# The first batch's v by quarters, with the preparation of the weights dealt out anew

## Chip, core and metric

The kernel runs on one core of a Trainium2 chip. The metric is the device time of one execution in microseconds; before the change it is 2723.61 us, the median of 3 runs (2723.01 to 2725.67).

## What is computed

The input x has shape (4, 1024, 32, 32) in float32: four batches of 1024 channels by 1024 tokens. Two layers follow each other. The first is attention over tokens, the second three convolutions with batch norms. The change lies in the first:

```
qkv = x @ w_qkv.T + b_qkv            # q, k, v: 1024 x 1024 weights each
q, k = rms_norm(rope(q)), rms_norm(rope(k))      # norm over all 1024 features
attn = softmax(q @ k.T * 64 ** -0.5)             # 16 heads of 64
out = rms_norm((attn @ v) @ w_proj.T) + x
```

So each batch has four products of 1024 x 1024 by 1024 x 1024: q, k, v and, after attention, the projection, called y in the kernel. Everything is float32. The second layer is 1x1, 3x3 and 1x1 convolution, each with a batch norm over all batches, and a residual.

## The kernel before

**Order of the stages.** The loop over b (L1000) takes one batch at a time through q, k, v, attention and y. The second layer follows after the last batch. In the profiled execution the stages of the first batch begin at 5 us (q), 103 (k), 204 (v), 319 (attention) and 554 (y); those of the second at 639 (q), 725 (k), 812 (v) and 897 (attention).

**One level and two levels.** The products of 1024 x 1024 matrices use a scheme of Strassen's kind: a matrix is cut into 2 x 2 blocks, and 7 products of blocks replace 8, at the price of sums of blocks ahead of the products (S1 to S4 of the weights, as many of the data) and of sums of results behind them. `project` (L290) does this once: 7 block products, each in 4 groups of output rows, so 28 steps. For q and k such a step is 4 matmuls with 512 columns; for v, which is wanted with tokens on the partitions (`tokens`), it is 16 matmuls with 128 columns each (L309 to L315). The profile counts each float32 matmul as two records. `project2` (L452) does it twice: each of the 7 outer products (their operands are listed in OUTER) is again done by 7 products of quarters, so 49 steps of 4 matmuls with 256 columns. Before the change the first batch's q, k and v use `project`; all else uses `project2`.

**The weights for two levels.** Each outer product k of `project2` needs seven weight quarters. Three are read as they are (`quarter`, L389); four are sums that were made once and stored in DRAM, in `wd2` (L147). A *weight part* is the making of these for one weight and one k (`prepare`, L400): four loads of 256 KB, four sums of 128 x 512 on VectorE (DVE), four stores of 256 KB through POOL's queue. Outer operands other than A11, A12 and A22 are themselves sums of blocks, which are read from `wd` (L145). In the first batch `operands` (L224), called by `project` for each of its 4 groups, loads four blocks through SP's queue, makes these sums on DVE, uses them for its own product, and stores them in `wd` through POOL's queue. For the projection's weights `prepare_blocks` (L416) makes them alone, in four steps.

**When the parts are made.** There are 28 weight parts (four weights, seven k). Before the change they are dealt out over the first batch:
- first q: q's and v's parts 0, 1, 6 and k's 0, 6, in the free tile `unused` (L1011)
- first k: q's 2, 3, 4, 5, in `room`, the tile that v will fill (L1021)
- first v: k's 1 to 5, in the half of x that v's products no longer need (L1029)
- first attention: four block sums and seven parts of the projection's weights, and v's 2, 3, 4, 5 (L1037)

In the projection stages a part is run by `weight_parts` (L966): loads through POOL's queue at a set point, sums `lag` steps later. The clock for this is `pace["at"]`, which `product_done` (L257) moves by 1 for each step of `project` and by 0.5 for each of `project2`. In attention a part is an `extra` step: after each of the 16 head pairs (two halves of the queries, eight pairs of heads each) one step is popped (L821 to L824), which makes the sums of the part loaded before and loads the next, through SP's queue, into four chunks of the weight ring.

**Other queues and buffers.** `wring` (L157) is a ring of 8 chunks of 256 KB for weights. It serves the matmuls' weights, `operands`, and the parts made in attention. A chunk is loaded again when the work on it, stores included, has ended. DVE also does the rotations (`turn`, L724), eight per q or k after the norm; each has two operations of 128 x 1024 and two accumulating DMAs on POOL's queue (L734). They wait in `waiting` and are taken out as the pace allows. `rest` (L272) takes out what is left before attention: in the first batch all of it, later all but 4, which are then taken out after the first head pairs. The instructions of TensorE, DVE, ScalarE (ACT) and POOL keep the order of the program; those of SP are ordered by the framework.

`in_place` (L659) gives `project2` its rooms for the sums of the data: parts of the destination at first, of x later. `project2` with `first` makes the sums of its first outer product itself (L542).

Of the kernel before, what the change touches and what calls it, by code (L numbers as in the profile page):

```python
# [12 lines left out]
AF = mybir.ActivationFunctionType  # L13
ALU = mybir.AluOpType
# [71 lines left out]
def program(ctx, tc, x, wblk, w2, w3, vecs, cos, sin, out, bad):  # L86
# [66 lines left out]
    with tc.tile_pool(name=f"st{u}", bufs=2) as st, ExitStack() as s:  # L153
# [58 lines left out]
        def chunk(name):  # L212
            return wring.tile([P, NH, P], F32, tag="w", name=name)

        def flat(t):
            return t.rearrange("p a b -> p (a b)")
# [6 lines left out]

        def operands(b, base, g, name):  # L224


            at = base // NT * NG + g
            if b > 0:
                out = [chunk(f"w_{name}_{o}") for o in SUMS]
                for o, t in enumerate(out):  # L230
                    nc.sync.dma_start(flat(t), wd[at, o])
                return out + [block(base, g + NG, 1, f"{name}_21")]
            a11, a12 = (block(base, g, ih, f"{name}_1{ih}") for ih in range(2))
            a21, a22 = (block(base, g + NG, ih, f"{name}_2{ih}") for ih in range(2))
            s1 = chunk(f"w_{name}_s1")
            nc.vector.tensor_tensor(s1, a21, a22, ALU.add)
            nc.vector.tensor_tensor(a21, a11, a21, ALU.subtract)
            nc.vector.tensor_tensor(a11, s1, a11, ALU.subtract)
            nc.vector.tensor_tensor(a12, a12, a11, ALU.subtract)
            spend(4 * TT)  # L240
            for o, t in enumerate((a11, s1, a21, a12)):
                nc.gpsimd.dma_start(wd[at, o], flat(t))
            return [a11, s1, a21, a12, a22]
# [45 lines left out]

        def project(b, base, bs, ts, outs, bias, squares, tokens, tag, w1=None):  # L290

# [8 lines left out]
            def product(o, w, name, first, last):  # L300
                r = right[name]
                if not tokens:
                    for i in range(NH):
                        nc.tensor.matmul(
                            o, w[:, i, :], r(i), start=first and i == 0, stop=last and i == NH - 1,
                            skip_group_check=True,
                        )
                    return
                for t in range(CH // P):  # L309
                    at = slice(t * P, (t + 1) * P)  # L310
                    for i in range(NH):
                        nc.tensor.matmul(
                            o[:, at], r(i)[:, at], w[:, i, :], start=first and t == 0 and i == 0,
                            stop=last and i == NH - 1, skip_group_check=True,
                        )  # L315

            def shaped(o):
                return o.rearrange("p (t f) -> p t f", f=P) if tokens else o

            def take(out, o, c):  # L320

                if bias is None or c is None:
                    nc.scalar.copy(out, shaped(o))
                else:
                    nc.scalar.activation(out, o, AF.Identity, bias=col(bias, c))

            def add(out, o, c):
                spend(TT)
                if bias is None:
                    nc.vector.tensor_tensor(out, shaped(o), out, ALU.add)  # L330
                else:
                    nc.vector.scalar_tensor_tensor(out, o, col(bias, c), out, ALU.add, ALU.add)

            def add_sbuf(out, t):
                spend(TT)
                nc.vector.tensor_tensor(out, shaped(t), out, ALU.add)

# [8 lines left out]
            for g in range(NG):  # L346
                c11 = outs(g)[0]
                o2 = bank("o2", f"pb_{tag}_{b}_{g}")
                product(o2, w1[NG + g], "A12", True, True)
                after(1, lambda o2=o2, c11=c11, g=g: add(c11, o2, g))  # L350
                after(2, lambda c11=c11: squares(c11, 0))
                product_done()
                if g == 1:
                    w2[0] = operands(b, base, 0, f"{tag}_{b}_0b")
            for g in range(NG):
# [8 lines left out]
                p5 = temp(f"p5_{n}")  # L364
                nc.scalar.activation(p5, o2, AF.Identity, bias=col(bias, g + NG)) if bias else nc.scalar.copy(p5, o2)
                product_done()
                if g + 1 < NG:
                    w2[g + 1] = operands(b, base, g + 1, f"{tag}_{b}_{g + 1}b")
                product(o, w[2], "S3", False, False)
# [29 lines left out]

        def prepare(which, base, k, alloc, queue=nc.sync):  # L400

# [13 lines left out]

        def prepare_blocks(base, g, alloc, queue=nc.sync):  # L416

# [171 lines left out]
        def qk_proj(b, base, bs, ts, bias, dst, tag, w1=None, two=None, bias_later=False):  # L589
# [22 lines left out]
            if two is None:  # L612
                project(b, base, bs, ts, outs, bias, squares, False, tag, w1)
                return total
# [15 lines left out]
            return total  # L630

        def v_proj(b, bs, ts, v, two=None):

            if two is not None:
                project2(b, 1, WV, *two, v, True, "v", lambda c: None)
                return

            def outs(g):
                n = N // P // 2
                return [  # L640
                    v[:, c * n : (c + 1) * n, f * P : (f + 1) * P] for f in (g, g + NG) for c in range(NCH)
                ]

            project(b, WV, bs, ts, outs, None, lambda *a, **k: None, True, "v")

# [128 lines left out]
        def attention(b, c, q_all, k_all, v, probs_, late, ready, extra, slow):  # L774
# [4 lines left out]
            for hp in range(NHP):  # L779
# [39 lines left out]
                if slow:  # L819
                    slow.pop(0)()  # L820
                if waiting:  # L821
                    next_waiting()
                elif extra:
                    extra.pop(0)()  # L824
# [141 lines left out]
        def weight_parts(parts, first, step, lag, alloc):  # L966

            for i, (which, base, k) in enumerate(parts):

                def begin(which=which, base=base, k=k):  # L970
                    after(lag, prepare(which, base, k, alloc, nc.gpsimd))

                after(first + i * step, begin)

        def pieces_of(tile, cols=NCH):

            at = deque(tile[:, i, h] for i in range(NT) for h in half[:cols])

            def alloc(name):
                at.rotate(-4)  # L980
                return [at[i] for i in range(-4, 0)]

            return alloc

        vector_and_act = {mybir.EngineType.DVE, mybir.EngineType.Activation}
# [14 lines left out]
        for b in range(B):  # L1000
# [8 lines left out]
            if b == 0:  # L1009
                unused = kp.tile([P, NT, N], F32, tag="k", name="unused")  # L1010
                parts = [(which, base, k) for which, base in ((0, WQ), (1, WV)) for k in (0, 1, 6)]  # L1011
                parts += [(3, WK, k) for k in (0, 6)]
                weight_parts(parts, 8, 2.4, 4, pieces_of(unused))
            tq = qk_proj(b, WQ, xs[b], ts[b], "bq", q_all, "q", w1 if b == 0 else None, two, True)
            rope(b, q_all, tq, eps_q, HD / C, None, "q", b == 0)
# [4 lines left out]
            if b == 0:  # L1020
                parts = [(0, WQ, k) for k in (2, 3, 4, 5)]  # L1021
                weight_parts(parts, 2, 5, 4, pieces_of(room))
            tk = qk_proj(b, WK, xs[b], ts[b], "bk", k_all, "k", None, two)
            rope(b, k_all, tk, eps_rms, 1.0 / C, (wqk_other, wqk), "k")
            v = room
            if b == 0:

                free = pieces_of(xs[b][:, :, half[0]], 1)
                weight_parts([(3, WK, k) for k in range(1, len(OUTER) - 1)], 8.5, 3, 3, free)  # L1029
            v_proj(b, xs[b], ts[b], v, (*two2[2], False) if b > 0 else None)  # L1030

            rest(leave=4 if b > 0 else 0)
            psum_for("att")

            todo = []
            if b == 0:
                todo = [lambda g=g: prepare_blocks(WP, g, pieces) for g in range(NG)]  # L1037
                todo += [
                    lambda which=which, base=base, k=k: prepare(which, base, k, pieces)
                    for which, base, ks in ((2, WP, (0, 1, 6, 2, 3, 4, 5)), (1, WV, (2, 3, 4, 5)))  # L1040
                    for k in ks
                ]
            made = []

            def extra_step():
                if made:
                    made.pop()()
                if todo:
                    made.append(todo.pop(0)())

# [48 lines left out]
            else:  # L1099
                back = {1: x_tile(b + 1)}  # L1100
                for i in range(NT):
                    after(8 + 1.5 * i, lambda i=i: read_back(1, (i,)))
            yt[b] = kp.tile([P, NT, N], F32, tag="k", name=f"y_{b}")
            two = (2, *in_place(q_all, tc_, yt[b], False), True)
# [357 lines left out]
```

## Time and profile before

| what | value |
|---|---|
| median of 3 runs | 2723.61 us |
| profiled execution: its time, its span | 2724.17 us, 2722.3 us |
| mean granted TensorE clock | 0.996 |
| DMA | 442.84 MB, mean 163 GB/s |
| DVE line L802 (sums of the softmax) | 470.4 us in 384 instructions |
| ACT line L798 (exponentials) | 476.2 us in 512 instructions |
| first v, records of 128 columns, 896 | from 204.26 us to attention at 319.05 us |
| second v, records of 256 columns, 392 | from 811.58 us to attention at 897.42 us |

The span is from the first to the last instruction of the one profiled execution; the execution's own time is 1.87 us longer. An instruction's duration is from its own start to its end, and matmuls overlap in the array: their rate is read from start to start. Idle time stands ahead of the instruction that ended it, with what released it. The releaser is inferred from semaphores.

### The profile page before, as it was taken

The numbers are of one execution on the slowest core, as the hardware profiler recorded it, in microseconds if no ns is written. First come the engines' busy times: TensorE is split into PE (matmuls) and PEld (weight loads), VectorE is DVE, ScalarE is ACT, GpSimd is POOL, SyncE is SP. The second block draws the span as 40 slices with busy tenths as digits, with TensorE's granted clock in tenths as the row PEclk, the third lists the DMA queues.
The fourth block names the chain that finished last, engine by engine and source line by source line (L and its number), as shares of the span: only waits on it lengthen the run. The fifth ranks groups of instructions, "written<-read, shape, count | busy, mean of one in ns | idle before, by whom it ended". The sixth has DMA issues, their size and how long they took to land. (4 is left out here: it accounts for less than half of the span.)

```text
span 2722.3 us, 33404 instructions
## 1 busy us (share of the span) xinstructions
PE 2679.2 (98%) x11914; PEld 1684.0 (62%) x11914; DVE 2129.7 (78%) x2461; ACT 1088.2 (40%) x1507; POOL 444.4 (16%) x536
## 2 busy tenths in 40 slices
PE   9999899999999999999999999999999999999997
PEld 4449633378888433588886333888884335846843
DVE  5565599988797877888888877887888878646987
ACT  2221255523343555433343555233425654312266
POOL 3553323210011121100111211100111211000000
PEclk9999999999999999999999999999999999999999
DMA  7896745576677332356666330665783323672165
GB/s 272 318 279 182 233 155 167 155 221 197 181 189 210 83 78 47 113 169 220 181 186 168 70 71 17 201 197 180 189 232 90 64 46 122 188 255 85 62 224 210
DMA packets 238399, 442.84 MB, mean 163 GB/s; under 512 B 27728, under 2 KB 111232, under 8 KB 238224
## 3 DMA queue, kind: packets, MB, share of 16 engines
q1 hardware_dynamic: 197280, 304.17, 35.7%
q0 software_dynamic: 40944, 136.44, 19.1%
q8 instruction: 98, 1.61, 0.2%
q14 instruction: 77, 0.63, 0.1%
HBM read 305.97 MB, written 96.78 MB: 148 GB/s over the span
## 5 line engine op out<-in xcount | busy, mean ns | idle before, releaser
L802 DVE TENSOR_TENSOR den<-den,p 128x1024 f32<-128x1024 f32 x384 | 470.4, 1225 | 41.4 <-ACT p L798 1.4
L798 ACT ACTIVATE p<-sc 128x1024 f32<-128x1024 f32 x512 | 476.2, 1043 | 53.7 <-PE sc L791 53.6
L791 PE MATMUL sc<-q,k 64*128 64x512 f32 x2048 | 457.9, 596 | 1.9 <-ACT p L798 1.2
L791 PEld LDWEIGHTS sc<-q,k 64*128 64x128 f32 x2048 | 190.1, 186 | 267.3 <-issue 121.1
L808 PE MATMUL cx<-p,to 128*64 128x512 f32 x1536 | 340.2, 595 | 0.0
L808 PEld LDWEIGHTS cx<-p,to 128*64 128x64 f32 x1536 | 106.0, 137 | 228.3 <-issue 228.3
L772 POOL TENSOR_SCALAR q<-q,vec 128x512 f32<-128x512 f32 x64 | 127.4, 1996 | 561.0 <-DVE q L771 561.0
L478 PE MATMUL p_y<-q,w_y 128*128 128x256 f32 x928 | 209.8, 379 | 0.0
L478 PEld LDWEIGHTS p_y<-q,w_y 128*128 128x128 f32 x928 | 176.0, 190 | 27.1 <-issue 3.4
L813 ACT COPY q<-cx 128x512 f32<-128x512 f32 x64 | 37.5, 587 | 357.0 <-PE cx L808 357.0
L473 PE MATMUL p_v<-w_v,x 128*128 128x256 f32 x696 | 157.9, 379 | 1.8 <-DVE x L444 1.7
L478 PE MATMUL p_k<-to,w_k 128*128 128x256 f32 x672 | 153.1, 381 | 3.2 <-ACT to L567 3.2
L478 PE MATMUL p_q<-to,w_q 128*128 128x256 f32 x672 | 152.5, 380 | 0.1
L800 DVE TENSOR_TENSOR den<-p 128x1024 f32<-128x1024 f32 x64 | 76.5, 1195 | 89.3 <-ACT p L798 89.3
L473 PEld LDWEIGHTS p_v<-w_v,x 128*128 128x128 f32 x696 | 132.0, 190 | 20.8 <-DVE x L444 3.0
L478 PEld LDWEIGHTS p_k<-to,w_k 128*128 128x128 f32 x672 | 126.7, 190 | 24.3 <-ACT to L567 5.6
L478 PEld LDWEIGHTS p_q<-to,w_q 128*128 128x128 f32 x672 | 127.2, 190 | 19.6 <-ACT q L532 1.3
L837 DVE RECIPROCAL rec<-dn 128x512 f32<-128x512 f32 x32 | 107.2, 3351 | 20.4 <-PE dn L831 20.3
L808 PE MATMUL cx<-p,rq 128*64 128x512 f32 x512 | 113.4, 595 | 0.0
L1366 PE MATMUL c<-h,w 128*128 128x512 f32 x256 | 110.3, 592 | 0.9 <-ACT h L1268 0.9
L734 POOL DMA_DIRECT2D k<-ks x64 | 56.9, 1099 | 243.1 <-ACT p L798 95.8
L478 PE MATMUL p_y<-to,w_y 128*128 128x256 f32 x384 | 90.1, 379 | 0.0
(475 smaller groups left out, 4264.0 us busy)
## 6 DMA issues: line engine op xcount, KB each, us to landing
w_y<-wd2f SPq DMA_DIRECT2D x112, 256.0 KB
w_q<-wd2f SPq DMA_DIRECT2D x84, 256.0 KB
w_k<-wd2f SPq DMA_DIRECT2D x84, 256.0 KB
w_v<-wd2f SPq DMA_DIRECT2D x84, 256.0 KB
x<-in_x_dram SPq DMA_DIRECT2D x64, 256.0 KB
q<-qs POOLq DMA_DIRECT2D x64, 256.0 KB, 5.5
k<-ks POOLq DMA_DIRECT2D x64, 256.0 KB, 4.5
inv<-rec SPq DMA_DIRECT2D x256, 64.0 KB
```

What stands on the lines that cost most here:

```text
L473: nc.tensor.matmul(o[:, q].rearrange("p (g f) -> p g f", g=2), r[:, i, q * P : (q + 1) * P], wt[:, :, i, :], skip_group_check=True, **at,)
L478: nc.tensor.matmul(o[:, q], wt[:, q, i, :], r[:, i, :], skip_group_check=True, **at)
L734: nc.gpsimd.dma_start(dst[i::2, f, :], other[1 - i :: 2, :], accum_op=ALU.add)
L772: nc.gpsimd.tensor_scalar(cx, cx, col("bv", hp), None, ALU.add)
L791: nc.tensor.matmul(sc[:, j], k_all[d, hp, t * P : (t + 1) * P], q_all[d, hp, at], start=True, stop=bad is not None,)
L798: nc.scalar.activation(p, sc, AF.Exp)
L800: nc.vector.tensor_tensor(d_, probs[0], p, ALU.add)
L802: nc.vector.tensor_tensor(d_, d_, p, ALU.add)
L808: nc.tensor.matmul(o[j * HD : (j + 1) * HD, :], v[:, t, h0 : h0 + HD], probs[t][:, j], start=(t == 0), stop=(t == N // P - 1),)
L813: nc.scalar.copy(q_all[:, hp, at], o)
L837: nc.vector.reciprocal(r, dn)
L1366: nc.tensor.matmul(os[i], w3t[k][f // NH][:, f % NH, :], h2[b, k][:, half[c]], start=(k == 0), stop=(k == NPT - 1),)
```

## The change

The first batch's v goes through `project2` like the others, with `first` set. `project` loses its case for tokens, and `operands` the case for later batches. The sums of blocks of v's weights, which `operands` made inside the first v, are made by four steps of `prepare_blocks` in the first q. v's seven parts have to be ready by the first v, so the other parts move later:
- first q: v's four block sums, then v's parts 0, 1, 6, 2
- first k: v's 3, 4, 5, then q's 0, 1 (five where four were)
- first v: q's 6, 2, in `ts[0][1]`, one of the tiles for sums of x
- first attention: the projection's as before, then q's 3, 4, 5 and k's 0
- first y: k's 1; second q: k's 2, 3, 4; second k: k's 5, 6

Two rotations may be left over when the first attention begins. There, an extra step now also runs beside a waiting one when the extra steps would otherwise not all fit.

```diff
-            project(b, WV, bs, ts, outs, None, lambda *a, **k: None, True, "v")
...
-                if waiting:
+                left = (NCH - c) * NHP - hp
+                turn = bool(waiting)
+                if turn:
                     next_waiting()
-                elif extra:
+                if extra and (not turn or len(extra) >= left):
                     extra.pop(0)()
...
-            for i, (which, base, k) in enumerate(parts):
-
-                def begin(which=which, base=base, k=k):
-                    after(lag, prepare(which, base, k, alloc, nc.gpsimd))
-
-                after(first + i * step, begin)
+            for i, part in enumerate(parts):
+                after(first + i * step, lambda part=part: after(lag, part(alloc, nc.gpsimd)))
...
+        def blocks_of(base):
+            return [lambda alloc, queue, g=g: prepare_blocks(base, g, alloc, queue) for g in range(NG)]
...
-                parts = [(which, base, k) for which, base in ((0, WQ), (1, WV)) for k in (0, 1, 6)]
-                parts += [(3, WK, k) for k in (0, 6)]
+                parts = blocks_of(WV) + [parts_of[WV][k] for k in (0, 1, 6, 2)]
                 weight_parts(parts, 8, 2.4, 4, pieces_of(unused))
+            elif b == 1:
+                weight_parts([parts_of[WK][k] for k in (2, 3, 4)], 1, 4.5, 4, pieces_of(room[:, : NT // 2, :]))
...
-                parts = [(0, WQ, k) for k in (2, 3, 4, 5)]
-                weight_parts(parts, 2, 5, 4, pieces_of(room))
+                parts = [parts_of[WV][k] for k in (3, 4, 5)] + [parts_of[WQ][k] for k in (0, 1)]
+                weight_parts(parts, 2, 4.5, 4, pieces_of(room))
+            elif b == 1:
+                weight_parts([parts_of[WK][k] for k in (5, 6)], 1, 5, 4, pieces_of(room[:, : NT // 2, :]))
...
-                free = pieces_of(xs[b][:, :, half[0]], 1)
-                weight_parts([(3, WK, k) for k in range(1, len(OUTER) - 1)], 8.5, 3, 3, free)
-            v_proj(b, xs[b], ts[b], v, (*two2[2], False) if b > 0 else None)
-
-            rest(leave=4 if b > 0 else 0)
+                two2 = [None, None, in_place(xs[b], ts[b], room, True)]
+
+                weight_parts([parts_of[WQ][k] for k in (6, 2)], 11.5, 6.5, 4, pieces_of(ts[b][1], 1))
+            project2(b, 1, WV, *two2[2], b == 0, v, True, "v", lambda c: None)
+
+            rest(leave=4 if b > 0 else 2)
...
-                todo = [lambda g=g: prepare_blocks(WP, g, pieces) for g in range(NG)]
-                todo += [
-                    lambda which=which, base=base, k=k: prepare(which, base, k, pieces)
-                    for which, base, ks in ((2, WP, (0, 1, 6, 2, 3, 4, 5)), (1, WV, (2, 3, 4, 5)))
-                    for k in ks
-                ]
+                todo = blocks_of(WP) + [parts_of[WP][k] for k in (0, 1, 6, 2, 3, 4, 5)]
+                todo += [parts_of[WQ][k] for k in (3, 4, 5)] + [parts_of[WK][0]]
...
+            if b == 0:
+                weight_parts([parts_of[WK][1]], 2, 0, 4, pieces_of(room[:, 3 * NT // 4 :, :]))
             yt[b] = kp.tile([P, NT, N], F32, tag="k", name=f"y_{b}")
```

More of the change, by code (lines that the diff above doesn't have):

```diff
@@ L222, in block, with operands @@
             return t
-        def operands(b, base, g, name):
+        def operands(base, g, name):
             at = base // NT * NG + g
[L228 to L232, printed above, removed]
             a11, a12 = (block(base, g, ih, f"{name}_1{ih}") for ih in range(2))
@@ L288, in queue_sums, with project @@
                 waiting.append((7 * TT, lambda i=i: sums(ts, bs, i)))
-        def project(b, base, bs, ts, outs, bias, squares, tokens, tag, w1=None):
+        def project(b, base, bs, ts, outs, bias, squares, tag, w1=None):
             right = {
@@ L301, in product @@
                 r = right[name]
[L302 to L318, printed above, removed]
+                for i in range(NH):
+                    nc.tensor.matmul(
+                        o, w[:, i, :], r(i), start=first and i == 0, stop=last and i == NH - 1,
+                        skip_group_check=True,
+                    )
             def take(out, o, c):
-                if bias is None or c is None:
-                    nc.scalar.copy(out, shaped(o))
+                if c is None:
+                    nc.scalar.copy(out, o)
                 else:
@@ L328, in add @@
                 spend(TT)
[L329 to L332, printed above, removed]
+                nc.vector.scalar_tensor_tensor(out, o, col(bias, c), out, ALU.add, ALU.add)
             def add_sbuf(out, t):
                 spend(TT)
-                nc.vector.tensor_tensor(out, shaped(t), out, ALU.add)
+                nc.vector.tensor_tensor(out, t, out, ALU.add)
             if w1 is None:
@@ L353, in project @@
                 if g == 1:
-                    w2[0] = operands(b, base, 0, f"{tag}_{b}_0b")
+                    w2[0] = operands(base, 0, f"{tag}_{b}_0b")
             for g in range(NG):
@@ L364, in project @@
                 p5 = temp(f"p5_{n}")
-                nc.scalar.activation(p5, o2, AF.Identity, bias=col(bias, g + NG)) if bias else nc.scalar.copy(p5, o2)
+                nc.scalar.activation(p5, o2, AF.Identity, bias=col(bias, g + NG))
                 product_done()
                 if g + 1 < NG:
-                    w2[g + 1] = operands(b, base, g + 1, f"{tag}_{b}_{g + 1}b")
+                    w2[g + 1] = operands(base, g + 1, f"{tag}_{b}_{g + 1}b")
                 product(o, w[2], "S3", False, False)
@@ L398, in quarter, with prepare @@
             queue.dma_start(t.rearrange("p (g f) -> p g f", g=2), src.rearrange("g p f -> p g f"))
-        def prepare(which, base, k, alloc, queue=nc.sync):
+        def prepare(which, base, k, alloc, queue):
             a11, a12, a21, a22 = a = alloc(f"pre_{which}_{k}")
@@ L414, in prepare, with prepare_blocks @@
             return make
-        def prepare_blocks(base, g, alloc, queue=nc.sync):
+        def prepare_blocks(base, g, alloc, queue):
             a11, a12, a21, a22 = a = alloc(f"blk_{base}_{g}")
@@ L612, in qk_proj @@
             if two is None:
-                project(b, base, bs, ts, outs, bias, squares, False, tag, w1)
+                project(b, base, bs, ts, outs, bias, squares, tag, w1)
                 return total
@@ L630, in qk_proj @@
             return total
[L632 to L641, printed above, removed]
-                ]
-            project(b, WV, bs, ts, outs, None, lambda *a, **k: None, True, "v")
         def operand(bs, ts):
@@ L966, in weight_parts @@
         def weight_parts(parts, first, step, lag, alloc):
-            for i, (which, base, k) in enumerate(parts):
-                def begin(which=which, base=base, k=k):
-                    after(lag, prepare(which, base, k, alloc, nc.gpsimd))
-                after(first + i * step, begin)
+            for i, part in enumerate(parts):
+                after(first + i * step, lambda part=part: after(lag, part(alloc, nc.gpsimd)))
         def pieces_of(tile, cols=NCH):
-            at = deque(tile[:, i, h] for i in range(NT) for h in half[:cols])
+            at = deque(tile[:, i, h] for i in range(tile.shape[1]) for h in half[:cols])
             def alloc(name):
@@ L983, in pieces_of @@
             return alloc
+        parts_of = {
+            base: [
+                lambda alloc, queue, which=which, base=base, k=k: prepare(which, base, k, alloc, queue)
+                for k in range(len(OUTER))
+            ]
+            for which, base in enumerate((WQ, WV, WP, WK))
+        }
+        def blocks_of(base):
+            return [lambda alloc, queue, g=g: prepare_blocks(base, g, alloc, queue) for g in range(NG)]
         vector_and_act = {mybir.EngineType.DVE, mybir.EngineType.Activation}
@@ L1036, in program @@
             if b == 0:
-                todo = [lambda g=g: prepare_blocks(WP, g, pieces) for g in range(NG)]
-                todo += [
-                    lambda which=which, base=base, k=k: prepare(which, base, k, pieces)
-                    for which, base, ks in ((2, WP, (0, 1, 6, 2, 3, 4, 5)), (1, WV, (2, 3, 4, 5)))
-                    for k in ks
-                ]
+                todo = blocks_of(WP) + [parts_of[WP][k] for k in (0, 1, 6, 2, 3, 4, 5)]
+                todo += [parts_of[WQ][k] for k in (3, 4, 5)] + [parts_of[WK][0]]
             made = []
@@ L1048, in extra_step @@
                 if todo:
-                    made.append(todo.pop(0)())
+                    made.append(todo.pop(0)(pieces, nc.sync))
             extra = [extra_step] * len(todo)
```

## The prediction

> **What bounds the kernel now.** I read the page's busy totals first, then its chain.
>
> ```profile
> PE 2679.2 (98%) x11914; PEld 1684.0 (62%) x11914; DVE 2129.7 (78%) x2461; ACT 1088.2 (40%) x1507; POOL 444.4 (16%) x536
> ```
>
> TensorE (PE) is busy for 98% of the 2722.3 us span. Time can only come from fewer or longer-streaming matmuls, or from the 43 us in which PE stands. So I went through PE's timeline in order of time, stage by stage. This is a stall in the first k, then the first v up to attention:
>
> ```profile
> 168.12 5.40 PE L304 MATMUL pa_k<-t,w_k_2b 128*128 128x512 f32 x8 [2.10 <-DVE w_k_2b L238]
> ...
> 204.26 14.45 PE L312 MATMUL pa_v<-w_v,x 128*128 128x128 f32 x128
> ...
> 233.60 3.74 PE L312 MATMUL pa_v<-w_v_0b,t 128*128 128x128 f32 x32
> 237.18 3.74 PE L312 MATMUL pc_v<-w_v_0b_s,t 128*128 128x128 f32 x32
> ...
> 278.65 5.35 PE L312 MATMUL pa_v<-w_v_2b,t 128*128 128x128 f32 x32 [9.15 <-DVE w_v_2b L238]
> ...
> 300.24 3.84 PE L312 MATMUL pa_v<-w_v_3b,t 128*128 128x128 f32 x32 [1.95 <-DVE w_v_3b L238]
> ...
> 319.05 2.85 PE L791 MATMUL sc<-q,k 64*128 64x512 f32 x12 [0.68 <-ACT rq L323]
> 323.13 4.79 PE L791 MATMUL sc<-q,k 64*128 64x512 f32 x20 [1.24 <-ACT p L798]
> 327.85 7.09 PE L808 MATMUL cx<-p,rq 128*64 128x512 f32 x32
> ```
>
> Columns are start, length, group, count and, in brackets, idle time before it with its releaser. A full group of 32 starts every 3.57 us: 111.7 ns per record (the durations overlap, so I use start to start). PE stood 9.15 and 1.95 us for weight sums that DVE makes (L236 to L239), and restarted slowly (5.35 us where 3.74 is normal; in k, eight records took 5.40 where 3.60 is normal). Second, the same projection in the second batch, already by quarters:
>
> ```profile
> 811.58 3.62 PE L473 MATMUL p_v<-w_v,x 128*128 128x256 f32 x16
> 815.03 3.62 PE L473 MATMUL p_v<-w_v,to 128*128 128x256 f32 x16
> ...
> 897.42 7.24 PE L791 MATMUL sc<-q,k 64*128 64x512 f32 x32
> 904.60 5.80 PE L808 MATMUL cx<-p,to 128*64 128x512 f32 x26
> ```
>
> Sixteen records in 3.45 us are 216 ns each, a product of eight 1.73 us, and nothing stands between v and attention. Last, stage windows, for what runs beside PE:
>
> ```profile
> 155.00:180.00 25.00, 22.90 (x50) 9.82 (x49) 18.71 (x23) 5.13 (x8) 15.78 (x23) 0.93 1.00 274
> 264.00:294.00 30.00, 20.85 (x174) 20.66 (x172) 14.56 (x18) 2.35 (x4) 20.80 (x31) 0.83 1.03 300
> 668.00:696.00 28.00, 28.00 (x131) 24.66 (x130) 26.13 (x34) 9.62 (x17) 3.15 (x6) 1.00 0.86 292
> ```
>
> After the window and its length come busy us of PE, weight loads, DVE, ACT and POOL, then granted clock, DMA share, GB/s. PE stands where the DMA share reaches 1.0 (second half of the first k, third quarter of the first v); the second q, by quarters, runs at share 0.86 without a gap.
>
> **First v, the gain.** Removed: 28 products of 32 records, 896 x 111.7 ns = 100.1 us. Added: 49 products of 8 records, 392; the second v's stage takes 85.84 us from 811.58 to 897.42, 0.57 of it a sum for k's norm that both have, so 85.3. Matmuls give 14.8 us. The rest is standing: first v to first cx is 327.85 - 204.26 = 123.59 us now, and 904.60 - 811.58 = 93.02 in the second batch. If the first v runs like the second the gain is 30.6 us: 14.8 from matmuls, 15.8 from stalls, slow restarts and the rough entry into attention. The releaser of those stalls, operands (16 sums on DVE, 16 writes on POOL inside v), goes from v altogether; block sums of v take its place in the first q, where eight steps at the same places (8 + 2.4 i) replace eight: equal loads, sums and writes, so I cost them at nothing; no cover is needed.
>
> **First k.** Four parts become five. A part is 4 loads and 4 writes of 0.26 MB and 4 DVE sums: 4 x 0.69 = 2.8 us of DVE, busy there for 65 of 101 us, 4 x 0.72 + 4 x 0.55 = 5.1 us of POOL issue, and 2.1 MB, at 297 GB/s (POOL's queue in the first v: 20.43 MB in 59.8% of 115 us) 7 us of DMA. k's DMA share is already 1.0 from 129 to 180 us. There DVE waited 5.60 us for the landing of a rotation of q, so made w_k_2b late, and PE stood 2.10 us and restarted 1.8 slow. POOL's queue is in order: behind the new part wait k's own sums (L242), whose landing frees chunks for SP's weight loads, and q's rotations. Bounds: -4 (that stall goes) to +6 (another like it and a half). I take +1, as the early parts move by only 0.5 to 1.5 products. The fifth part's buffers are where v's first inner sums are written: made at product 24 of 28, some 13 us before v, it needs 3 for sums and 6 to land. Cost 0 to 3, taken in v.
>
> **DMA in the first v.** Weights are 49 x 0.262 = 12.9 MB instead of 6.3; two q parts bring 4.2, the part left from k 1.05, the four blocks' first loads 2.1; rotations, tables and norm stay 5.8. That is 26 MB, up to 3 of which can slip into attention (share 0.27 in its first 28 us). At 300 GB/s (the row at share 1.03) it is 76 to 87 us of the 85.8. Now it is 26.9 MB in 115. So DMA goes from partly to fully taken, and here a rule speaks against the change. The Trainium skill, DMA: Bandwidth & Descriptors, section Queues, rings and completion order: each DMA engine takes the queues with work in turn, packet by packet. So while POOL's queue is full, SP's weights get about half, 150 GB/s, and they need 12.9 MB / 85.8 us = 150: by the rule no stall on average and no margin. By the rows, share 0.86 costs nothing and share 1.0 cost the first k 3.9 us per 25 us. I take 2 us, range 0 to 8, for POOL's bursts are single parts with rotations between them. Behind the second q part's loads, which wait on POOL for the first one's writes in the same four pieces (ts[1]), stand the last rotations of k; attention reads their heads late, and two are left for it anyway. DVE in v: the second v has 67.8 us of 86; two parts add 5.5, two rotations less take 5: no bound.
>
> **Attention and the second q and k.** Attention keeps 15 weight steps (three q and one k part for four of v: equal loads, sums and writes). Two rotations (5.1 us of DVE) go into the first two head pairs, where DVE is busy 19.6 of 28 us: hidden. But the weight steps then start one head pair later, and the last is made in the last pair instead of the one before. Now POOL issues its writes, and SP goes on with the loads that wait for its chunks, at (timelines of POOL and of SP):
>
> ```profile
> 542.76 2.13 POOL L412 DMA_DIRECT2D wd2f<-w_pre  x4 [13.43 <-DVE w_pre L410]
> ```
> ```profile
> 545.12 1.17 SPq L465 DMA_DIRECT2D w_y<-wd2f  x2
> ```
>
> That is 2.4 us from issue to landing. Afterwards the sums come after the two means (551.3 to 552.5), so at 555.4; POOL's two bias steps hold it until 556.8; writes land from 559.2; SP's loads of the sixth to eighth chunk of y's weights follow one by one to 561.9. The eighth, landing like the write 2.4 us later, is there at 564.3; y's fifth product needs it at 554.1 + 4 x 1.73 = 561.0. PE stands 3.3 us, with SP's order 0 to 6. Here a second rule: TensorE: Matmul & The Clock Gate, section Why this matters for your kernels, says that gaps over about 3 us between matmuls send the clock to half. By it a gap of 3.3 is at the edge, free or with a slow restart of some 1.6 (as after the 9.15), and one of 2.10 free. The trace is harsher: 2.10 us in k cost 1.8 more, though 1.95 in v only 0.1. The longer row is the nearer: y costs 3.3 + 1.7 = 5 us (0 to 8).
>
> In the second q three k parts add 8.3 us to DVE (68 of 85.5) and in k two add 5.5 (73 of 87). Where the tightest is emitted, the inner sums that follow end at 674.7 in q and 761.4 in k (DVE's timeline), and PE needs them with product 23, at 638.8 + 0.6 + 23 x 1.73 = 679.2 and 764.9: 4.5 and 3.5 us to spare, and 2.8 fits both. The last k part is made at product 10 of k's 24.5, and its weights are loaded after 15. DMA gets 6.3 MB more in q, 4.2 in k (shares 0.5 to 0.86). I take 0.5 us, 0 to 4. Only one part goes into the first y (2.8 us of DVE at some 575 us); PE, already late there, covers it; without that cover 2.
>
> **Sum.** 2722.3 - 30.6 + 1 + 2 + 5 + 0.5 = 2700.2 us of span. The profiled execution took 2724.17, 1.87 beyond its span and 0.56 over the median 2723.61: 2700.2 + 1.87 - 0.56 = 2701.5.
>
> **Rivals.**
> 1. Nothing new stands: first v like the second, y's chunks in time. 2723.6 - 30.6 = 2693, to 2697. For it: quarters at 292 GB/s without a gap. Against: y's chunk order. Chance 0.20.
> 2. The waits come back in part: k +5, v +6, y +7, second q and k +2 make 20 of the 30.6: 2713 (2706 to 2718). For it: share 1.0 in both stages. Chance 0.20.
> 3. Slower: v becomes DMA-bound. Its 26 MB at the rate that POOL's queue has in the second v, mostly rotations (4.2 MB in 22.1% of 89 us, 213 GB/s), take 122 us, 36 over 85.8: 2693 + 36 + 6.5 = 2735. It decides from 225 GB/s down (26 MB in 115 us: 2693 + 29.5 + 6.5 = 2729). Against: full windows moved 274 and 300. Chance 0.02.
> 4. It does little: the same between 225 and 249 GB/s, 2718 to 2729. Chance 0.03.
>
> My forecast (2697 to 2706) has 0.55. A measurement can tell some 0.2% (5.4 us) from no change; so faster 0.95, same 0.03, slower 0.02. The range takes in rival 1 and most of rival 2: 2694 to 2712.
>
> **What would show it.** Right: v with 392 records at 216 ns, 86 to 90 us long, nothing before attention's first scores; a gap of about 3 us in y's first ten products, released by a weight load; DMA share over 0.9 in v. Wrong: gaps in v released by w_v loads or by inner sums (L444); k's gap grown beyond 6 us; gaps in the second q or k at L444. No gap in y would make it rival 1.

## The result and the profile after

The changed kernel takes 2713.53 us (median of 9 runs, 2710.92 to 2719.32) beside 2724.28 for the kernel before (9 runs on the same chips). The ratio is 0.9966, with a 95% interval of 0.9956 to 0.9976: faster by 10.8 us, where 22 were forecast. The range given (2694 to 2712) missed it by 1.5 us. The profiled execution took 2712.96 us, with a span of 2711.0.

First the page's busy totals after the change:

```profile
PE 2665.8 (98%) x11410; PEld 1658.3 (61%) x11410; DVE 2171.9 (80%) x2516; ACT 1096.3 (40%) x1520; POOL 448.5 (17%) x552
```

There are 504 fewer matmul records, as counted, and DVE has 42 us more to do. Then PE's timeline (start, length, group, count, idle time before it and its releaser), in the first v:

```profile
203.41 3.62 PE L453 MATMUL p_v<-w_v,x 128*128 128x256 f32 x16
...
287.38 1.89 PE L453 MATMUL p_v<-w_v,x 128*128 128x256 f32 x8
289.19 7.25 PE L757 MATMUL sc<-q,k 64*128 64x512 f32 x32
296.37 7.09 PE L774 MATMUL cx<-p,rq 128*64 128x512 f32 x32
```

No group between them has idle time before it. From the first v matmul to the first cx it is 92.96 us, where it was 123.59. So the first v gained its 30.6 us in full. They were given back later. This table is made from the starts of the stages' first matmuls in the same view:

| stage | before, us | after, us |
|---|---|---|
| first q | 97.9 | 98.1 |
| first k | 101.0 | 99.4 |
| first v, up to cx | 123.6 | 93.0 |
| first attention, cx to y | 226.3 | 226.3 |
| first y | 84.7 | 95.9 |
| second q | 85.7 | 92.7 |
| second k | 87.1 | 89.8 |
| second v | 85.8 | 85.5 |

Three stages lost 11.2 + 7.0 + 2.7 = 20.9 us. With the 30.6 and 1.6 us that the first v and k gained, 11.3 us are left, which is the difference of the two spans (2722.3 and 2711.0). Here is where PE stands in the three stages:

```profile
522.63 3.72 PE L458 MATMUL p_y<-q,w_y 128*128 128x256 f32 x16
526.19 1.89 PE L458 MATMUL p_y<-y,w_y 128*128 128x256 f32 x8
530.47 1.99 PE L458 MATMUL p_y<-y,w_y 128*128 128x256 f32 x8 [2.39 <-DVE rec L805]
537.26 3.75 PE L458 MATMUL p_y<-q,w_y 128*128 128x256 f32 x8 [4.80 <-DMA w_y<-in_wblk_dram]
540.81 2.61 PE L458 MATMUL p_y<-y,w_y 128*128 128x256 f32 x8
543.26 3.62 PE L458 MATMUL p_y<-q,w_y 128*128 128x256 f32 x16
...
655.20 3.50 PE L458 MATMUL p_q<-x,w_q 128*128 128x256 f32 x8 [4.38 <-DMA w_q<-wdf]
744.97 1.97 PE L458 MATMUL p_k<-x,w_k 128*128 128x256 f32 x8 [1.77 <-DMA w_k<-wdf]
```

A product of eight records has 1.73 us when nothing is in its way. From 537.26 two products took 6.00 us, 2.5 too many: after the gap of 4.80 us PE restarted slowly. The windows of the two places (length, then busy us of PE, weight loads, DVE, ACT, POOL, then granted clock, DMA share, GB/s) show why:

```profile
529.00:533.00 4.00, 1.99 (x8) 1.44 (x8) 3.90 (x4) 0.50 (x1) 0.91 (x2) 1.00 0.96 277
533.00:537.00 4.00, 0.00 (x0) 0.00 (x0) 3.96 (x6) 0.09 (x1) 0.00 (x0) 0.80 1.04 352
537.00:541.00 4.00, 3.74 (x9) 3.05 (x10) 1.91 (x4) 0.00 (x0) 0.54 (x1) 0.50 0.57 128
...
645.00:660.00 15.00, 10.62 (x42) 8.79 (x42) 14.42 (x19) 4.28 (x8) 6.09 (x11) 0.89 1.02 372
```

PE stands with the DMA engines full (share 0.96 to 1.04), and the granted clock is 0.50 in the 4 us after the gap in y.

### The profile page after: what moved, and what is told of

The parts are those of the page before. It is cut to its first block, busy times and chain, and to the rows that moved or that the text cites. A ratio compares the mean times of both kernels' runs of the same rounds, so it can differ in the third digit from the quotient of the medians.

```text
span 2711.0 us, 32574 instructions
## 1 busy us (share of the span) xinstructions
PE 2665.8 (98%) x11410; PEld 1658.3 (61%) x11410; DVE 2171.9 (80%) x2516; ACT 1096.3 (40%) x1520; POOL 448.5 (17%) x552
## 5 line engine op out<-in xcount | busy, mean ns | idle before, releaser
L453 PE MATMUL p_v<-w_v,x 128*128 128x256 f32 x928 | 209.7, 379 | 1.0 <-DVE x L424 1.0
L453 PEld LDWEIGHTS p_v<-w_v,x 128*128 128x128 f32 x928 | 176.2, 190 | 25.8 <-DVE x L424 1.4
```

Of the source, the lines that this page charges most:

```text
L453: nc.tensor.matmul(o[:, q].rearrange("p (g f) -> p g f", g=2), r[:, i, q * P : (q + 1) * P], wt[:, :, i, :], skip_group_check=True, **at,)
```

## The experiments

The theory: y stands because the last weight step of attention now comes in the last head pair, so that its sums hold up the reciprocal (`rec`) and its stores hold up the chunks for y's weights; the second q stands because the loads and stores of k's parts meet the stores of the first y's norm on the DMA engines. Rivals: y stands for the k part whose loads begin with y; q stands because DVE is late. Each experiment is an edit of the changed kernel. Before each stands what was on record ahead of the run.

**1. Weight steps from the first head pair on.**

```diff
-                if extra and (not turn or len(extra) >= left):
+                if extra:
```

> Only change against the changed kernel: in attention an extra weight step runs after every head pair, also beside a left-over rotation, so the last step ends one head pair before the end, as before the change. Theory (the first y stands for two reasons that both come from the late last step: its sums delay the reciprocal that holds a PSUM bank, and its stores delay the chunks for y's weights): the gap of 2.4 us released by the reciprocal and the gap of 4.8 us released by a weight load both go, with the slow restart, and the first y takes 85 to 88 us in place of 95.9; time 8 to 11 us less than the changed kernel, about 2704. Rival (the stand comes from the k part whose loads begin with y): y keeps the 4.8 us gap and takes 92 us or more; time at most 4 us less.

The first y took 86.0 us, within 85 to 88. PE's timeline in y:

```profile
523.49 3.72 PE L458 MATMUL p_y<-q,w_y 128*128 128x256 f32 x16
527.05 3.62 PE L458 MATMUL p_y<-y,w_y 128*128 128x256 f32 x16
530.50 1.89 PE L458 MATMUL p_y<-q,w_y 128*128 128x256 f32 x8
...
543.75 1.99 PE L458 MATMUL p_y<-to,w_y 128*128 128x256 f32 x8 [1.01 <-DMA w_y<-wdf]
```

Both gaps are gone, with the k part still there. DVE ended `rec` at 524.70 + 3.35 = 528.05 us, and y's fourth product, which waited for it, falls due at 523.49 + 3 x 1.73 = 528.7. In the changed kernel `rec` ended at 530.41, due at 527.8. The wait of PE for `rec` is what the trace shows; that it is for a PSUM bank (attention's banks become the projection's) is read from the code. The total missed its expectation and fell into the rival's: 2713.75 us (ratio 0.9964, 0.9950 to 0.9978), no better than the changed kernel, though the second attention began 9.4 us earlier in the profiled execution. The edit also took effect in the last batch, where the extra steps are the filters' sums: they moved beside the rotations, and that attention took 241.3 us in place of 234.0:

```profile
2090.68 1.05 PE L799 MATMUL dn<-den,ones 128*32 128x512 f32 x4 [0.51 <-DVE den L768]
...
2124.01 1.05 PE L799 MATMUL dn<-den,ones 128*32 128x512 f32 x4 [2.85 <-DVE den L768]
```

DVE was late with the softmax sums (`den`), so PE stood. The two gaps make 3.4 of the 7.3 us, and the slow restart behind the second makes 1.7 (34 records in 8.77 us, where 7.07 is normal).

**2. The first y's k part later.**

```diff
-                weight_parts([parts_of[WK][1]], 2, 0, 4, pieces_of(room[:, 3 * NT // 4 :, :]))
+                weight_parts([parts_of[WK][1]], 10, 0, 4, pieces_of(room[:, 3 * NT // 4 :, :]))
```

> Only change: the k part in the first y begins at step 10 in place of 2; the late last weight step stays. Theory (late last step): the gap released by the reciprocal stays at 2.4 us, the one released by the weight load shrinks by 1 to 3 us because its landing is no longer beside four other loads, y takes 91 to 95 us. Rival (the k part's loads): the gap released by the weight load goes and y takes 86 to 89 us.

```profile
531.17 1.99 PE L458 MATMUL p_y<-y,w_y 128*128 128x256 f32 x8 [2.40 <-DVE rec L805]
535.40 2.58 PE L458 MATMUL p_y<-q,w_y 128*128 128x256 f32 x8 [2.24 <-DMA w_y<-in_wblk_dram]
537.78 3.00 PE L458 MATMUL p_y<-y,w_y 128*128 128x256 f32 x8
```

y took 91.5 us: the theory's case. The gap for `rec` stays, the other falls from 4.80 to 2.24 us, and the slow restart from 2.5 to 1.8. Without the late step (experiment 1) y lost 1.3 us, without the part's early loads it lost 6.8. So the late step is needed for all of y's loss but 1.3 us, and the part's loads beside it made it worse by 4.3. The total was 2712.04 us (ratio 0.9963, 0.9949 to 0.9977), which can't be told from the changed kernel's.

**3 and 4. The second q's parts with their DMAs alone, and with their sums alone.** A part in the second q became, in turn:

```diff
             def make():
-                nc.vector.tensor_tensor(a22, a21, a22, ALU.add)
...
                 for m, t in enumerate((a11, a22, a21, a12)):
                     nc.gpsimd.dma_start(wd2[which, k, m], t)
```
```diff
-            for i, t in enumerate(a):
-                quarter(t, base, k, i // 2, i % 2, queue)
...
-                for m, t in enumerate((a11, a22, a21, a12)):
-                    nc.gpsimd.dma_start(wd2[which, k, m], t)
```

> The four sums of each of the second q's three k parts are left out (their loads and stores stay, so later k products read unsummed weights). Theory (the second q stands because the parts' loads and stores meet the stores of the first y's norm): the gap of 4.4 us and its slow restart stay, the second q takes 91 to 93 us as in the changed kernel (92.7). Rival (VectorE is late with the inner sums): it takes 86 to 87 us.

> The loads and stores of the second q's three k parts are left out, their sums stay (on whatever lies in the pieces; k's products read part 1's stored sums in their place). Theory (DMA): no gap released by a weight load, the second q takes 86 to 87 us. Rival (VectorE): 91 to 93 us, with gaps released by inner sums.

Each ran once (2713.34 and 2707.63 us), so only the stage is read here. The second q took 92.7 us with the DMAs alone and 85.7 with the sums alone: all of its loss is due to the DMAs. The four kernels that keep the three parts where the change put them (the changed one, experiments 1, 2 and 5) have 92.7 to 95.4 us there. PE's timeline, DMAs alone, then sums alone:

```profile
656.05 3.38 PE L470 MATMUL p_q<-x,w_q 128*128 128x256 f32 x8 [4.58 <-DMA w_q<-wdf]
```
```profile
653.10 1.89 PE L470 MATMUL p_q<-x,w_q 128*128 128x256 f32 x8
```

One more rival can be read from SP's timeline: that SP issued the weight loads late. These are its last loads of this kind before the product where PE stood, in the changed kernel and with the sums alone:

```profile
642.21 3.81 SPq L378 DMA_DIRECT2D w_q<-wdf  x3
```
```profile
644.66 3.81 SPq L378 DMA_DIRECT2D w_q<-wdf  x3
```

Both are 23.71 us behind the first product of the stage (618.50 and 620.95). So SP was on time, and the loads landed late.

**5. The first edit, in the first batch alone.**

```diff
-                if extra and (not turn or len(extra) >= left):
+                if extra and (not turn or b == 0 or len(extra) >= left):
```

> As the first experiment, but the extra step runs beside a left-over rotation in the first batch alone, since in the last batch the same edit also moved the filters' sums into the first head pairs and its attention took 241.3 us in place of 234.0. Theory (that attention is all that hid the gain): first y 86 us, second q still 93, last attention 234; 2701 to 2705 us, 8 to 11 below the changed kernel. Rival (the time given back in y returns elsewhere whatever one does): 2710 or more.

2706.0 us (2705.35 to 2708.32; ratio 0.9939, 0.9925 to 0.9952), y 85.7 us, the last attention 234.0. The median is 1 us outside what was expected. In the profiled execution (2707.12 us) the second q took 95.4 us, where 93 had been expected: its gaps, 3.55 and 2.28 us, are of the same kind.

**6. k's parts apart from the norm's stores.**

```diff
-                weight_parts([parts_of[WK][k] for k in (2, 3, 4)], 1, 4.5, 4, pieces_of(room[:, : NT // 2, :]))
+                odd = pieces_of(room[:, : NT // 2, half[1]], 1)
+                weight_parts([parts_of[WK][2]], 0.5, 0, 4, odd)
+                weight_parts([parts_of[WK][3]], 2, 0, 4, pieces_of(room[:, : NT // 2, half[0]], 1))
+                weight_parts([parts_of[WK][4]], 14, 0, 4, odd)
...
-                weight_parts([parts_of[WK][1]], 2, 0, 4, pieces_of(room[:, 3 * NT // 4 :, :]))
+                weight_parts([parts_of[WK][1]], 6, 0, 4, pieces_of(room[:, 3 * NT // 4 :, :]))
```

> The fifth experiment, and the k parts of the second q are kept away from the stores of the first y's norm: parts 2 and 3 are loaded and made early (steps 0.5 and 2, sums at 4.5 and 6), part 4 late (14, sums at 18), in pieces that are free then; the first y's part begins at step 6. The DMA bytes of q stay the same. Theory (a collision in time with the norm's stores): second q 86 to 88 us, total 2694 to 2699. Rival (the second q has too many DMA bytes in all): q stays at 91 or more, total 2700 to 2705.

```profile
646.34 1.96 PE L458 MATMUL p_q<-x,w_q 128*128 128x256 f32 x8
```

The product before which PE had stood now comes without a gap, and the second q took 86.7 us. The bytes were not quite the same, against what was expected: POOL issued the loads of two of the three parts in the first y already, where the changed kernel did so with one. So the stage moved 21.80 MB, where it had moved 22.85 in the changed kernel and 17.68 before. A fifth of the added bytes went, and of a loss of 9.7 us (experiment 5) only 1.0 stayed: it was mainly the collision in time. The total, 2701.17 us (2699.19 to 2704.66; ratio 0.9917, 0.9903 to 0.9930), is 2 us above what the theory expected and in the rival's range. In its profiled execution (2704.66, the highest of the five) the second k took 91.8 and the first k 102.1 us.

**7. Two of k's parts in the first y, two early in the second q.**

```diff
-                weight_parts([parts_of[WK][k] for k in (2, 3, 4)], 1, 4.5, 4, pieces_of(room[:, : NT // 2, :]))
+                weight_parts([parts_of[WK][k] for k in (3, 4)], 0.5, 1.5, 4, pieces_of(room[:, : NT // 2, :]))
...
-                weight_parts([parts_of[WK][1]], 2, 0, 4, pieces_of(room[:, 3 * NT // 4 :, :]))
+                weight_parts([parts_of[WK][k] for k in (1, 2)], 6, 7, 4, pieces_of(room[:, 3 * NT // 4 :, :]))
```

> The fifth experiment with two k parts in the first y (steps 6 and 13) and two in the second q, both early (0.5 and 2). Theory: second q 86 to 87 us, first y 85 to 88, total 2693 to 2698. Rival (VectorE or DMA is full in y then): y 90 or more, total above 2700.

y took 85.8, q 87.0, k 89.2 us; the total was 2701.66 us (2699.01 to 2703.09; ratio 0.9921, 0.9907 to 0.9934), in the rival's range, though y and q were the theory's. Experiments 6 and 7 can't be told apart, and both are faster than the kernel before and the changed kernel.

**8. Without k's parts 1 to 6.** Experiment 5 without them:

> The fifth experiment with k's parts 1 to 6 left out altogether (k's products read part 0's stored sums in their place), so that the first y, second q and second k have only the work of before. Theory (the parts' DMA in these three stages and the late step are all that was lost): stages at 84.7, 85.7 and 87.1 us, total 2691 to 2695, the 30.6 us of the first v in full. Rival (something else in the change costs too): 2698 or more.

2694.79 us (2694.18 to 2697.16; ratio 0.9899, 0.9884 to 0.9914). y, q and k took 85.6, 85.7 and 87.1 us. So the parts in these three stages and the late step account for nearly all of the loss: 28.9 of the 30.6 us are there in the total (the kernel before took 2723.68 us beside it). In the profiled execution y is still 0.9 us longer than before, and the first attention took 227.4 us in place of 226.3, as in all kernels whose weight steps run from the first head pair on. The parts were taken out whole; DMAs and sums were told apart in the second q alone (experiments 3 and 4).

**9. The second k's parts early too.** Experiment 7 and:

```diff
-                weight_parts([parts_of[WK][k] for k in (5, 6)], 1, 5, 4, pieces_of(room[:, : NT // 2, :]))
+                weight_parts([parts_of[WK][k] for k in (5, 6)], 0.5, 1.5, 4, pieces_of(room[:, : NT // 2, :]))
```

> The seventh experiment, and the two k parts of the second k are loaded early as well (steps 0.5 and 2 in place of 1 and 6), ahead of the rotations of q whose DMAs fill the middle of that stage. Theory (loads that meet other DMA in time): the gap of 2 us released by a weight load in the second k goes, k takes 87 to 88 us in place of 89.2, total 1 to 2 us less than the seventh, about 2700. Rival (the parts' bytes cost the same wherever they lie in k): 89 us, no change.

A miss: k took 90.7 us, the total 2703.43 (2699.68 to 2705.92; ratio 0.9923, 0.9909 to 0.9938).

```profile
730.54 1.97 PE L458 MATMUL p_k<-x,w_k 128*128 128x256 f32 x8 [0.76 <-DMA w_k<-wdf]
...
740.15 5.02 PE L458 MATMUL p_k<-to,w_k 128*128 128x256 f32 x22 [2.47 <-ACT k L547]
```

The gap for a weight load fell from 1.98 to 0.76 us, but a new one came. DVE's waits in the same stretch name what is late next:

```profile
DVE sinT L688 <- DMA sqq<-inv_df: 4.1, 1, 4.1
```

In experiment 7 this wait is 0.9 us. POOL now issues the first part's stores at 713.09 us, right ahead of the two DMAs that send the norm of q round (716.07 and 720.38); in experiment 7 the stores come behind these. That they hold the norm up, and DVE's queue behind it, is read from this order and not shown by a run of its own. Neither of the two places tried for two parts in k costs nothing.

## Why the prediction was half right

- **First v: right.** PE ran 392 records at 216 ns each, and 30.6 us came off between the first v and the first cx. The 2 us taken for DMA did not come: PE ran without a gap at a share of 1.01 (247 to 268 us).
- **First k: wrong in sign, small.** +1 was taken, -1.6 measured: two gaps of 0.58 and 1.34 us in place of one of 2.10 with its slow restart. Among the runs of the experiments this stage took 99.1 to 102.1 us.
- **First y: the mechanism was right, the size wrong.** The step said that the eighth chunk, "landing like the write 2.4 us later", makes PE stand 3.3 us, with 1.7 for the restart: 5. It was 11.2: 2.4 for `rec`, 4.8 for the load, 2.5 for the restart, the rest smaller gaps. Two terms failed. The first is `rec`, which the sum put at nothing: it followed the stores and loads of the late step, and did not ask what the step's own four sums hold up on DVE. `rec` stands behind them in the same queue, and before the change it had 0.6 us to spare. The second is the landing, which was taken from a write that began with DMA idle (share 0.00 in the 2.7 us before). SP issued the loads in question here:

```profile
528.88 2.29 SPq L378 DMA_DIRECT2D w_y<-in_wblk_dram  x3
```

  PE went on at 537.26, 6.4 to 8.4 us later. In experiment 2 the same three were issued from 529.55 on, and PE went on at 535.40, after 2.5 us less. So the part's loads make 2.5 of the 4 to 6 us that the sum lacks; the rest is not explained. The sum had left them out. The program places them at step 2, behind four products, but POOL's queue had nothing to wait for and issued them at 527.02, 4.4 us after y began.
- **Second q and k: the step that failed most.** "I take 0.5 us, 0 to 4": 9.7 were lost. DMA was read from a mean over 28 us (share 0.86). In windows of 7 us of the kernel before, the share is already 0.99 when the first y's norm is stored:

```profile
667.00:674.00 7.00, 7.00 (x35) 6.15 (x34) 6.97 (x8) 4.00 (x7) 1.42 (x4) 1.00 0.99 346
```

  The parts were put on top of that. In the changed kernel the DMA view of 640 to 665 us has:

```profile
q0 software_dynamic: 1940, 6.70, 70.7%
q1 hardware_dynamic: 1812, 2.46, 30.0%
...
x1df<-y POOLq DMA_DIRECT2D x5, 512.0 KB, 9.5
to<-wdf POOLq DMA_DIRECT2D x8, 256.0 KB, 7.4
wd2f<-to POOLq DMA_DIRECT2D x7, 256.0 KB, 5.8
```

  Columns are packets, MB and share of the engines' time, then by transfer the count, size and us to landing. SP's weights (q1) moved 2.46 MB in 25 us, 98 GB/s, where PE needs 150. The rule that each DMA engine takes the queues with work in turn, packet by packet (the Trainium skill, DMA: Bandwidth & Descriptors, section Queues, rings and completion order), had been read as half of the engines for SP. From 247 to 268 us, in v, SP did have 49%, and PE ran on; here it had 30%. The rule counts packets, and of those SP had nearly half here, 1812 beside 1940; but one of SP's held 1.4 KB on average and one of POOL's 3.5. So even turns need not be even bytes. Shorter windows have other counts (774 beside 434 from 646 to 653 us), and how the engines choose is not shown; that the stores of the norm and the parts together were too much is (experiments 4 and 6). For the second k, where 2.7 us were lost, DMA is only read from what ended the gap of 1.77 us, a weight load.
- **DVE margins in q: right.** Sums alone cost nothing.
- **Clock.** In y the gap of 4.80 us cost 2.5 in slow products, at a granted clock of 0.50; in q 4.38 cost 1.6. The rule of the prediction (the Trainium skill, TensorE: Matmul & The Clock Gate, section Why this matters for your kernels: no gaps over about 3 us between matmuls) would make every shorter gap free. That holds for 2.47 us in experiment 9, and for 2.39 in y as far as the one product behind it shows (1.99 us long, where 1.89 is normal). It fails for 2.10 (before), 2.19 (experiment 4) and 2.61 us (experiment 6) in the first k, 2.24 in y (experiment 2, soon after the 2.40) and 2.28 in the second q (experiment 5): each cost 1.7 to 1.8 us. In these runs no gap under 2 us was followed by a slow restart, up to the second attention. So between 2 and 3 us both happened, and the length of the gap alone doesn't settle it; what does is not shown.

Rival 2 had the shape (y +7, second q and k +2, and 2713 us in all), but for other stages: it put 11 us on the first k and v, which lost nothing. That the range was missed by no more than 1.5 us is luck: in the first v and k together the sum had taken 4.6 us too many, and they hide as much of the 15 us that it lacked in y, q and k.

## What to carry to other kernels

Work that is moved off one stage lands on the DMA queues of another: look there in short windows (here 7 us), not at the stage's mean. When a step is put last before a change of stage, list everything that stands behind it in that engine's queue, and how much time each has to spare. A queue that waits for nothing runs ahead of the step at which the program issues to it.

## What had not been expected

A load of 256 KB from SP took at least 6.4 us to be used when POOL had four loads and four stores of the same size in flight (528.88 to 530.8 until 537.26). The runs of the changed kernel spread over 8.4 us (9 runs), those of the kernel before over 4.5 (9 runs), and those without k's parts over 3.0 (4 runs); that the gaps for DMA make the difference is not shown. One edit of a condition in attention, meant for the first batch, cost 7.3 us in the last one and hid the gain of experiment 1.
